# Keys of layers 2 and 3 stored with 32 rows per head and loaded in one piece per four heads; one batch's expert rows placed behind the other batch's norm

## The chip, the cores and the metric

One core of one Trainium2 chip runs the whole program. The metric is the device time in microseconds (us) of one execution; the time of a kernel is the median of three runs. Engines: PE (TensorE, matrix products), DVE (VectorE), ACT (ScalarE), POOL (GpSimd), SP (SyncE, which issues most DMA transfers). Each engine works through its own queue in order. 16 DMA engines move data between DRAM and the on-chip memory SBUF.

## The reference, cut to what matters

The network has four layers. Each adds a cross attention to a context of 2 x 1024 rows and then a feed-forward part to the residual rows `x` (2 batches of 512 rows of 256). The places of this change are layer 1's experts, layer 2's attention and layer 3's attention:

```python
x = x + tanh(g_xattn[1]) * L1_xattn(layernorm(x), ctx, ctx, ...)   # "attention 1": 16 heads of 8
x = x + tanh(g_ffn[1])   * L1_ffn(layernorm(x), Wg, bg, W1, W2)    # 8 experts, each row to one
x = x + tanh(g_xattn[2]) * L2_xattn(layernorm(x), ctx, ctx, ...)   # "attention 2": 16 heads of 16
x = x + tanh(g_ffn[2])   * L2_ffn(layernorm(x), ...)               # ternary weights
x = x + tanh(g_xattn[3]) * L3_xattn(layernorm(x), ctx, ctx, ...)   # "attention 3": 8 heads of 4
x = x + tanh(g_ffn[3])   * L3_ffn(layernorm(x), ...)
# an attention: softmax(q k^T * scale) v Wo, with q from layernorm(x) and k, v from ctx
```

## The kernel before, in words

The kernel is written in a tile framework. The program is traced as Python runs; a planner then puts the instructions of each engine in order, by what it reckons to be ready and by program order, gives buffers out and adds the semaphores. `keep_in_program_order` pins one instruction behind the one traced before it on the same engine; without it the planner may move it.

**Keys.** All keys are computed from the context ahead of their layer (`keys`, line 923) and written to DRAM tensors `K_l1`, `K_l2`, `K_l3` of shape [heads, head size + 1, 2048] (`prepare_context`, line 910). The extra row holds ones: the maximum of a score row is subtracted by way of it. An attention reads four heads at a time as a tile `KT` of 128 partitions x 2048 (`loaded_keys`, line 1013): head h of the four sits on partitions 32 h to 32 h + head size, and the rest must be zero. So `KT` is set to zero on POOL (line 1019), and four loads on SP (line 1021) bring the heads: 9 rows of 8 KB each for layer 1, 17 for layer 2, 5 for layer 3. There are 4, 4 and 2 such tiles.

`KT` lives in the buffers with the tag `wide`, of which there are four. The experts' weights `w1e` and `w2e` (1 MB each, lines 1306 and 1308) use the same four buffers, and the ternary part keeps half of its lowest split part and `w3` in them. A `KT` of layer 2 is therefore free to be filled only when the last experts have used their weights: the first when expert 6 is done with its first weight, the last at the end of the experts' last product.

**Experts.** `moe_ffn` (line 1300) sends each row to a place in DRAM by expert (`xg`, an indirect DMA from POOL), runs the experts one after another (`arrive`, `hidden`, `leave`; the output rows `ye` go from ACT's queue to `yg` in DRAM, line 1408), and asks for `KT` of layer 2 after the last. The rows come back in `rest` (line 1424), which attention 2 calls for each batch: four gathers from `yg` on POOL (line 1427), then four updates of `x` on DVE (line 1434).

**The start of an attention** (`attention`, line 1038). Batch 0's `rest` runs first. Then `queries(0)` and batch 1's `rest` are interleaved, one step of each in turn: `queries` begins with the row statistics (lines 156 to 168: statistics and aggregate per block on DVE, variance plus epsilon, square root on ACT, reciprocal and `nb` on DVE); the normalised rows `h` (line 184, ACT) are transposed on PE (line 1070), copied, and multiplied by the query weights (line 1076). Scores (line 1143), their maxima (DVE, lines 1150 and 1152), exponentials (1174, 1179) and values (1186) follow, group by group of four heads. `queries(1)` runs between the first scores.

**Attention 1's aside.** `prepare_routing` (line 1516) is called inside attention 1 after its first scores. It sets a tile `zero` (128 x 256) and stores it from SP over parts of `xg` and `yg` (2.5 MB, line 1524).

**The ternary part** (`ternary_ffn`, line 1582) calls `loads()` near its end: `KT` and values `V` of layer 3 (two loads of 1 MB, line 1032). Then comes a branch (line 1689) past a path in full precision that is not taken with these weights; every engine goes through it. Two more such branches are at lines 254 and 1364.

The interleaving that matters for the order of the updates:

```python
for _ in before(range(BPB), bank):
    pass
first, second = queries(0), before(range(BPB, NB), bank)
for _ in first:
    next(second, None)
for _ in second:
    pass
```

Of the kernel before, what the change touches and what calls it, by code (L numbers as in the profile page):

```python
# [20 lines left out]
F32 = mybir.dt.float32  # L21
# [4 lines left out]
ALU = mybir.AluOpType  # L26
# [3 lines left out]
B, S, D = 2, 512, 256  # L30
M = 1024
# [43 lines left out]
def _bc(ap, shape):  # L75

    return ap.broadcast_to(shape)


class _Net:  # L80
# [829 lines left out]
    def prepare_context(self):  # L910
        nc = self.nc
        self.kd, self.vd = {}, {}
        for name, H, HD in (("l1", 16, 8), ("l2", 16, 16), ("l3", 8, 4)):
            k = self.dram.tile([H, HD + 1, B * M], F32, name=f"K_{name}")
            self.kd[name] = k
            nc.sync.dma_start(
                k[:, HD, :].rearrange("h (c m) -> h c m", m=P),
                _bc(self.ones[:H].unsqueeze(1), [H, B * M // P, P]),
            )
        for name, H in (("l1", 16), ("l3", 8)):  # L920
            self.vd[name] = self.dram.tile([B * M, H * 32], F32, name=f"V_{name}")
# [88 lines left out]

        return V, self.by_key(wv, D, to), keys()

    def loaded_keys(self, name, H, HD):

        nc = self.nc
        KT = []
        for g in range(H // 4):
            k = self.wide("KT")([P, B, M])
            nc.gpsimd.memset(k, 0.0)  # L1019
            for h in range(4):  # L1020
                nc.sync.dma_start(
                    k[32 * h : 32 * h + HD + 1].rearrange("r b m -> r (b m)"),
                    self.kd[name][4 * g + h],
                )
            KT.append(k)
        return KT

# [10 lines left out]
    def attention(  # L1038
        self, name, KT, V, H, HD, scale, gate, before, bq=None, bv=None, bo=None, aside=None
    ):  # L1040
# [88 lines left out]
        def largest(u, ring=False):  # L1129
# [11 lines left out]
            for i in range(2):  # L1141
                r = 32 * (2 * pair + i)
                nc.tensor.matmul(  # L1143
                    sc[i], lhsT=QT[r : r + 32, g, (b * BPB + k) * P : (b * BPB + k + 1) * P],
                    rhs=KT[g][r : r + 32, b, ts(half, 512)], start=True, stop=True,
                )
# [153 lines left out]
    def moe_ffn(self, gate):  # L1300
        nc, d = self.nc, self.d
# [14 lines left out]
        rows = self.big.tile([P, NB, D], F32, tag="q", name="rows_h")  # L1316
        hT = self.hp.tile([P, DC, T], F32, tag="hT", name="hT")
        for n2 in range(NB // 2):
            tp = self.ps1.tile([P, DC, 2, P], F32, tag="one", name="tp")
            for k in range(2):  # L1320
                n = 2 * n2 + k
# [7 lines left out]
        p, dest, some, many = self.gates(gate, hT, wg, values)  # L1329
# [68 lines left out]
        def leave(e, h1, w2):  # L1398
            for t in range(2):
                ps = self.ps1.tile([HCAP, D], F32, tag="one", name="py")  # L1400
                for fc in range(HC):
                    nc.tensor.matmul(  # L1402
                        ps, lhsT=h1[:, fc, ts(t, HCAP)], rhs=w2[:, fc, :],
                        start=(fc == 0), stop=(fc == HC - 1),
                    )
                y = self.big.tile([HCAP, D], F32, tag="avj", name="ye", bufs=2)
                self.copy(y, ps)
                nc.scalar.dma_start(self.yg[e * CAP + t * HCAP : e * CAP + (t + 1) * HCAP], y)
# [10 lines left out]
            if e + 1 < NE and e + 1 not in ws:  # L1419
                ws[e + 1] = load(e + 1)  # L1420
        leave(*before)
        KT = self.loaded_keys("l2", 16, 16)

        def rest(blocks, bank):
            y = self.big.tile([P, BPB, D], F32, tag="e", name="yn", bufs=4)
            for k, n in enumerate(blocks):
                nc.gpsimd.indirect_dma_start(
                    out=y[:, k, :],
                    out_offset=None,
                    in_=self.yg[:, :],  # L1430
                    in_offset=bass.IndirectOffsetOnAxis(ap=dest[:, n : n + 1], axis=0),
                )
            for k, n in enumerate(blocks):
                nc.vector.scalar_tensor_tensor(
                    self.x[:, n, :], y[:, k, :], some[:, n : n + 1], self.x[:, n, :],
                    ALU.mult, ALU.add,
                )
                yield

# [76 lines left out]
    def prepare_routing(self):  # L1516

        nc = self.nc
        self.xg = self.dram.tile([NE * CAP + T, D], F32, name="xg")
        self.yg = self.dram.tile([NE * CAP + T, D], F32, name="yg")  # L1520
        zero = self.wk.tile([P, D], F32, tag="h", name="zero", bufs=2)
        nc.gpsimd.memset(zero, 0.0)
        for to, k in ((self.xg[: NE * CAP], NE * CAP // P), (self.yg[NE * CAP :], T // P)):
            nc.sync.dma_start(
                to.rearrange("(k p) f -> p k f", p=P), _bc(zero.unsqueeze(1), [P, k, D])
            )
        self.rank, self.first, self.behind = (
            self.const.tile([P, n], F32, name=name)
            for n, name in ((NE, "rank"), (NE, "first"), (NB, "behind"))
        )  # L1530
        for to, n, step, base, by in (
            (self.rank, NE, -1, NE, 0), (self.first, NE, CAP, 0, 0), (self.behind, NB, P, NE * CAP, 1)
        ):
            i = self.sm.tile([P, 8], I32, tag="ri", name="ri", bufs=1)
            nc.gpsimd.iota(i, pattern=[[step, n]], base=base, channel_multiplier=by)
            nc.vector.tensor_copy(to, i)

        self.upper = self.const.tile([P, P], F32, name="upper")
        nc.gpsimd.memset(self.upper, 1.0)
        nc.gpsimd.affine_select(  # L1540
            out=self.upper, in_=self.upper, pattern=[[1, P]], compare_op=ALU.is_gt, fill=0.0,
            base=0, channel_multiplier=-1,
        )
# [260 lines left out]
    def run(self):  # L1804
        ov = self.out.rearrange("(n p) f -> p n f", p=P)
        self.setup()
        self.sampled_attention()
        self.after_layer_0()
        kv = self.loaded_keys("l1", 16, 8), self.loaded_values("l1", 16)
        self.attention(  # L1810
            "l1", *kv, 16, 8, D**-0.5, 1, lambda blocks, bank: self.int8_ffn(4, blocks),
            aside=self.prepare_routing,
        )
        *kv, rest = self.moe_ffn(5)
        self.attention("l2", *kv, 16, 16, 0.25, 2, rest, "bq2", "bv2", "bo2")
        kv, rest = self.ternary_ffn(
            6, lambda: (self.loaded_keys("l3", 8, 4), self.loaded_values("l3", 8))
        )
        scale = float(np.float32(1.0) / np.sqrt(np.float32(32.0)))
        self.attention("l3", *kv, 8, 4, scale, 3, rest, "bq3", "bv3", "bo3")  # L1820
        self.channel_mix_ffn(
            7, lambda n: self.nc.sync.dma_start(ov[:, n, :], self.x[:, n, :])
        )
# [105 lines left out]
```

## Time and profile before

| | us |
|---|---|
| median of 3 runs (lowest, highest) | 1298.85 (1297.12, 1301.19) |
| the profiled execution | 1298.23 |
| its span | 1296.5 |
| PE busy in the span | 1156.7 (89%) |
| DVE, ACT, POOL busy | 720.3, 607.5, 228.3 |
| mean granted PE clock | 0.933 |
| `KT` memsets on POOL | 10 of 1.8 each |

The profile is of one execution: a span, the busy time of each engine, and groups of instructions by line with their mean duration and the idle time before them, with what ended it. A timeline lists instructions with start, duration, engine, line and tiles, and in brackets the idle time of the engine just before with its releaser. "out<-in" names tiles. A letter q behind an engine (SPq, PEq) is that engine's sequencer. In the tables by stretches of time each engine has its busy time in us and, in brackets, the instructions; then come the granted PE clock (1.00 is full), the busy share of the 16 DMA engines and GB/s.

### The profile page before, as it was taken

How to read it: one execution, taken by the hardware profiler on the slowest of the kernel's cores; microseconds unless marked ns; L12 is line 12 of the kernel's file. 1: busy time of each engine (PE TensorE's matmuls, PEld its weight loads, DVE VectorE, ACT ScalarE, POOL GpSimd, SP SyncE). 2: the span in 40 equal slices, each digit the busy share in tenths (PEclk: the TensorE clock that was granted, in tenths of full speed). 3: DMA queues.
4: the chain of work that ended last, by engine and by line, in shares of the span. 5: the costliest groups of instructions: out<-in, count | busy, mean ns of one | idle time of the engine just before them, and what ended most of it. 6: DMA issues, size and time to landing. Idle time of an engine off the chain costs nothing. (4 is left out here: it accounts for less than half of the span.)

```text
span 1296.5 us, 16857 instructions
## 1 busy us (share of the span) xinstructions
PE 1156.7 (89%) x6576; PEld 540.6 (42%) x6596; DVE 720.3 (56%) x1106; ACT 607.5 (47%) x1166; POOL 228.3 (18%) x204
## 2 busy tenths in 40 slices
PE   6987499999998989937999899969999997999977
PEld 3334333333334578823333233334444445543324
DVE  5794678787764111114788778448333111588635
ACT  2422236888874311103488678646333110258761
POOL 1043201334320200131033233000000000113200
PEclk9978698999999989977899999979999998989988
DMA  6033530000211345420000100000122112000000
GB/s 220 1 118 111 116 137 5 1 1 1 66 34 41 111 155 190 156 68 27 16 2 1 66 1 2 17 18 1 34 84 58 58 33 80 9 1 1 10 0 33
DMA packets 56837, 67.49 MB, mean 52 GB/s; under 512 B 4064, under 2 KB 45568, under 8 KB 56288
## 3 DMA queue, kind: packets, MB, share of 16 engines
q1 hardware_dynamic: 52856, 61.07, 15.0%
q0 software_dynamic: 896, 2.49, 0.7%
q10 hardware_dynamic: 2992, 2.70, 0.6%
q8 instruction: 57, 0.93, 0.3%
q14 instruction: 36, 0.29, 0.1%
HBM read 49.93 MB, written 16.32 MB: 51 GB/s over the span
## 5 line engine op out<-in xcount | busy, mean ns | idle before, releaser
L1152 DVE TENSOR_REDUCE part<-scores 128x2 f32<-128x1024 f32 x290 | 341.8, 1219 | 92.5 <-PE bank L1174 77.1
L1179 ACT ACTIVATE e<-bank 128x512 f32<-128x512 f32 x580 | 302.2, 601 | 121.1 <-PE bank L1174 89.4
L1174 PE MATMUL bank<-qa,KT 32*128 32x512 f32 x1160 | 306.1, 634 | 0.6 <-DVE o L1213 0.6
L1143 PE MATMUL scores<-KT,QT 32*128 32x512 f32 x1160 | 293.9, 641 | 4.2 <-DVE part L1152 4.2
L1198 POOL TENSOR_TENSOR avT<-avT,avj 128x512 f32<-128x512 f32 x113 | 143.2, 1268 | 345.9 <-ACT avj L1197 345.9
L1186 PE MATMUL bank<-e,V 128*32 128x512 f32 x1280 | 182.8, 607 | 2.5 <-ACT e L1179 2.5
L1143 PEld LDWEIGHTS scores<-KT,QT 32*128 32x128 f32 x1160 | 100.6, 190 | 157.3 <-DVE part L1152 115.3
L1634 PE MATMUL pg<-hid,wg_h 128*128 128x512 bf16 x752 | 165.1, 379 | 0.8
L1174 PEld LDWEIGHTS bank<-qa,KT 32*128 32x128 f32 x1160 | 117.2, 188 | 36.0 <-issue 18.2
L1634 PEld LDWEIGHTS <-wg_h 128*128 128x128 bf16 x768 | 75.1, 98 | 90.6
L1019 POOL MEMSET KT<- 128x2048 f32 x10 | 18.0, 1821 | 375.9 <-PE pg L1634 157.3
L1186 PEld LDWEIGHTS bank<-e,V 128*32 128x32 f32 x1280 | 28.3, 108 | 106.2 <-ACT e L1179 94.9
L1197 ACT COPY avj<-bank 128x512 f32<-128x512 f32 x113 | 69.2, 612 | 6.7 <-PE bank L1186 6.7
L1402 PE MATMUL py<-w2e,h 128*96 128x256 f32 x256 | 57.4, 379 | 0.0
L1596 DVE TENSOR_REDUCE low<-wg_h 128x1 f32<-128x1024 uint16 x16 | 19.5, 1217 | 57.1 <-DMA wg_h<-in_h2T 54.4
L1606 DVE TENSOR_TENSOR rest<-g,hid 128x512 f32<-128x512 f32 x32 | 21.2, 690 | 51.5 <-ACT hid L1605 51.3
L1070 PE MATMUL bank<-ident,h 128*128 128x128 f32 x48 | 11.7, 369 | 39.0 <-ACT h L184 32.2
L1402 PEld LDWEIGHTS py<-w2e,h 128*96 128x96 f32 x256 | 41.2, 163 | 12.2
L1386 PE MATMUL ph<-xeT,w1e 128*128 128x192 f32 x256 | 45.1, 337 | 0.0
L1386 PEld LDWEIGHTS ph<-xeT,w1e 128*128 128x128 f32 x256 | 43.6, 198 | 1.3 <-DVE xeT L109 0.6
L1076 PE MATMUL bank<-hT,w_l_wq 128*128 128x512 f32 x80 | 41.4, 644 | 2.1 <-DVE part L1150 1.4
L1667 ACT ACTIVATE hid<-pg,cols 128x512 f32<-128x512 f32 x16 | 10.1, 683 | 70.2 <-PE pg L1634 70.2
(303 smaller groups left out, 1325.2 us busy)
## 6 DMA issues: line engine op xcount, KB each, us to landing
w1e<-in_W SPq DMA_DIRECT2D x8, 1024.0 KB
w2e<-in_W SPq DMA_DIRECT2D x8, 1024.0 KB
V_l<-v1st SPq DMA_DIRECT2D x16, 256.0 KB
V<-V_l SPq DMA_DIRECT2D x2, 2048.0 KB
wg_h<-in_h1T SPq DMA_DIRECT2D x8, 512.0 KB
wg_h<-in_h2T SPq DMA_DIRECT2D x8, 512.0 KB
K_l<-kst SPq DMA_DIRECT2D x12, 256.0 KB
KT<-K_l SPq DMA_DIRECT2D x16, 136.0 KB
```

Of the source, the lines that this page charges most:

```text
L1076: nc.tensor.matmul(ps, lhsT=wq[:, dc, ts(c, P)], rhs=hT[:, dc, ts(b, S)], start=(dc == 0), stop=(dc == DC - 1),)
L1143: nc.tensor.matmul(sc[i], lhsT=QT[r : r + 32, g, (b * BPB + k) * P : (b * BPB + k + 1) * P], rhs=KT[g][r : r + 32, b, ts(half, 512)], star ...
L1152: nc.vector.tensor_reduce(to, both, AX.X, ALU.max, negate=True)
L1174: nc.tensor.matmul(t, lhsT=KT[g][r : r + 32, b, ts(j, P)], rhs=augmented[n][r : r + 32, :], start=True, stop=True,)
L1179: nc.scalar.activation(e[:, h, :], t, AF.Exp, scale=scale)
L1186: nc.tensor.matmul(po[32 * h : 32 * h + 32, :], lhsT=V[b][:, j, ts(4 * g + h, 32)], rhs=e[:, h, :], start=True, stop=True,)
L1197: nc.scalar.copy(t, po)
L1198: nc.gpsimd.tensor_tensor(part["oT"], part["oT"], t, ALU.add)
L1386: nc.tensor.matmul(ps[:, k // 2, k % 2, :CAP], lhsT=w1[:, dc, ts(4 * fp + k, P)], rhs=xeT[:, dc, :], start=(dc == 0), stop=(dc == DC - 1),)
L1402: nc.tensor.matmul(ps, lhsT=h1[:, fc, ts(t, HCAP)], rhs=w2[:, fc, :], start=(fc == 0), stop=(fc == HC - 1),)
L1606: nc.vector.tensor_tensor(r, g, hi, ALU.subtract)
L1634: nc.tensor.matmul(ps[:, ts(t, 512)], lhsT=w[:, c, ts(oc, P)], rhs=src(i, c, ts_(t, 512)), start=(c == 0 and i == 0), stop=(c == chunks - ...
```

## The change

Layers 2 and 3 get 32 rows per head in DRAM, so that four heads are 128 rows that lie one behind another: one load of 1 MB fills a whole `KT`, and the memset goes. The rows that were zeroed in SBUF before are now stored as zeros in DRAM, once, by three stores in `prepare_routing`, inside attention 1. Layer 1 stays as it was. Besides, the updates of batch 1 in the experts' `rest` are pinned in program order, which puts the first of them behind the last DVE instruction of batch 0's statistics (`nb`, line 168) and each other one behind the one before.

```diff
@@ prepare_context
-            k = self.dram.tile([H, HD + 1, B * M], F32, name=f"K_{name}")
+            rows = HD + 1 if name == "l1" else 32
+            k = self.dram.tile([H, rows, B * M], F32, name=f"K_{name}")
@@ loaded_keys
-    def loaded_keys(self, name, H, HD):
+    def loaded_keys(self, name, H):
...
             k = self.wide("KT")([P, B, M])
-            nc.gpsimd.memset(k, 0.0)
-            for h in range(4):
-                nc.sync.dma_start(
-                    k[32 * h : 32 * h + HD + 1].rearrange("r b m -> r (b m)"),
-                    self.kd[name][4 * g + h],
-                )
+            kd = self.kd[name][4 * g : 4 * g + 4]
+            flat = k.rearrange("p b m -> p (b m)")
+            if kd.shape[1] == 32:
+                nc.sync.dma_start(flat, kd.rearrange("h r m -> (h r) m"))
+            else:
+                nc.gpsimd.memset(k, 0.0)
+                for h in range(4):
+                    nc.sync.dma_start(flat[32 * h : 32 * h + kd.shape[1]], kd[h])
             KT.append(k)
@@ moe_ffn, rest
+            stay = self.tc.keep_in_program_order if blocks.start else lambda i: i
             for k, n in enumerate(blocks):
-                nc.vector.scalar_tensor_tensor(
-                    self.x[:, n, :], y[:, k, :], some[:, n : n + 1], self.x[:, n, :],
-                    ALU.mult, ALU.add,
+                stay(
+                    nc.vector.scalar_tensor_tensor(
+                        self.x[:, n, :], y[:, k, :], some[:, n : n + 1], self.x[:, n, :],
+                        ALU.mult, ALU.add,
+                    )
                 )
                 yield
@@ prepare_routing
+        for name, HD in (("l2", 16), ("l3", 4)):
+
+            for h in range(0, self.kd[name].shape[0], 8):
+                to = self.kd[name][h : h + 8, HD + 1 :, :]
+                nc.sync.dma_start(
+                    to.rearrange("h r m -> h (r m)").rearrange("h (c m) -> h c m", m=D),
+                    _bc(zero[:8].unsqueeze(1), [8, (31 - HD) * B * M // D, D]),
+                )
```

More of the change, by code (lines that the diff above doesn't have):

```diff
@@ L1421, in moe_ffn @@
         leave(*before)
-        KT = self.loaded_keys("l2", 16, 16)
+        KT = self.loaded_keys("l2", 16)
         def rest(blocks, bank):
@@ L1808, in run @@
         self.after_layer_0()
-        kv = self.loaded_keys("l1", 16, 8), self.loaded_values("l1", 16)
+        kv = self.loaded_keys("l1", 16), self.loaded_values("l1", 16)
         self.attention(
@@ L1816, in run @@
         kv, rest = self.ternary_ffn(
-            6, lambda: (self.loaded_keys("l3", 8, 4), self.loaded_values("l3", 8))
+            6, lambda: (self.loaded_keys("l3", 8), self.loaded_values("l3", 8))
         )
```

## The prediction

> **What bounds the kernel now.** I read the page first. TensorE (PE) is busy for 89% of a span of 1296.5 us; the program is a chain of stages on one core, and PE is the engine that ends most of them. So a change that touches no matmul can pay only where PE stands still. The slices show one such place outside the start: around 565 to 585 us, between the experts and attention 2. I took the timelines of each engine there, then the stretches of 1 us.
>
> PE's timeline: after the experts' last product (562.0) PE starts again with the transposes of attention 2's normalised rows.
>
> ```profile
> 587.31 1.18 PE L1070 MATMUL bank<-ident,h 128*128 128x128 f32 x4 [25.32 <-ACT h L184]
> ```
>
> 25.3 us are empty. What is in them, from the timelines of POOL, SP, DVE and ACT (start, duration, engine, line):
>
> ```profile
> 562.05 1.80 POOL L1019 MEMSET KT<- 128x2048 f32 x1 [5.10 <-PE py L1402]
> 569.92 1.05 POOL L1427 DMA_INDIRECT yn<-yg,gt  x1 [6.07 <-DMA KT<-K_l]
> ```
> ```profile
> 579.63 0.48 DVE L1434 SCALAR_TENSOR_TENSOR x<-yn,gt,x 128x256 f32<-128x256 f32 x1 [0.82 <-DMA yn<-yg,gt]
> ...
> 581.23 0.45 DVE L1434 SCALAR_TENSOR_TENSOR x<-yn,gt,x 128x256 f32<-128x256 f32 x1
> 581.60 0.17 DVE L157 BATCH_NORM_AGGREGATE mv<-st 128x2 f32<-128x6 f32 x1
> 581.92 0.48 DVE L1434 SCALAR_TENSOR_TENSOR x<-yn,gt,x 128x256 f32<-128x256 f32 x1
> 582.32 0.16 DVE L160 TENSOR_SCALAR rs<-mv 128x4 f32<-128x4 f32 x1
> 583.53 0.48 DVE L1434 SCALAR_TENSOR_TENSOR x<-yn,gt,x 128x256 f32<-128x256 f32 x1 [1.05 <-DMA yn<-yg,gt]
> 584.81 0.48 DVE L1434 SCALAR_TENSOR_TENSOR x<-yn,gt,x 128x256 f32<-128x256 f32 x1 [0.79 <-DMA yn<-yg,gt]
> ...
> 586.26 0.16 DVE L162 RECIPROCAL rs<-rs 128x4 f32<-128x4 f32 x1
> ...
> 586.48 0.14 DVE L168 SCALAR_TENSOR_TENSOR nb<-mv,rs 128x4 f32<-128x4 f32 x1
> ```
> ```profile
> 582.52 0.20 ACT L161 ACTIVATE rs<-rs 128x4 f32<-128x4 f32 x1 [18.42 <-DVE rs L160]
> 586.65 1.09 ACT L184 ACTIVATE h<-x,nb,rs 128x256 f32<-128x256 f32 x2 [3.93 <-DVE nb L168]
> ```
>
> Two holes are to be seen. POOL stands for 6.07 us before the first gather of expert rows, on a load of keys that the gather does not read. And ACT has the root of batch 0's variance at 582.72, but its reciprocal runs at 586.26: in front of it on DVE stand four updates of batch 1's rows (581.23 to 585.29), the last two waiting for gathers.
>
> Why the keys are slow, from the stretches of 1 us (after the engines: PE clock, DMA share, GB/s): the first is all keys, the second a weight load of 1 MB.
>
> ```profile
> 566.00:567.00 1.00, 0.00 (x0) 0.00 (x0) 0.00 (x0) 0.00 (x0) 0.00 (x0) 1.00 0.06 27
> ...
> 540.00:541.00 1.00, 1.00 (x6) 0.74 (x5) 0.00 (x0) 0.00 (x0) 0.00 (x0) 1.00 1.08 384
> ```
>
> A load of 17 rows (136 KB) fills 0.06 of the DMA engines, one of 16, at 25 to 27 GB/s: 5.3 us each, one after another. SP's issues agree (568.79, then 574.07). The 1 MB load was issued at 536.57 and its traffic is over at 542.0: 5.4 us.
>
> **The change, part by part.**
>
> *Zeros in attention 1.* Three more stores on SP behind those issued at 178.6 and 179.0: 16 heads x 15 rows x 8 KB + 8 x 27 x 8 KB = 3.7 MB, in pieces of 1 KB, out of 8 partitions. The existing zeros (2.5 MB, same pieces, 128 partitions) took 9 us, at 386 GB/s at best. Bounds: 14 us at that rate, 150 us if they went through one engine like the 17-row loads; so over by 195 to 330. Behind them on SP are a value weight (192.57; needed near 400) and expert weights (326). The moved transfers otherwise stay, and attention 1's DMA is idle (0 to 2 GB/s from 200 to 300). Cost: 0, cover over 70 us.
>
> *Keys of layer 2.* Gone: 4 memsets of 1.80 us on POOL and 16 loads of 136 KB; new: 4 loads of 1 MB straight behind the release of their buffers (542.4, 549.0, 555.1, 562.0). The first three land inside the experts' 12.5 us rhythm (two 1 MB weights each did so without delay for PE); the bytes double to 4 MB, and the scores that want the first group start only at 600.73. The fourth is issued at about 562.1 and lands at 562.1 + 5.4 = 567.5.
> The gather then waits for the last expert rows alone. Their store is issued at 562.5; its traffic shows at 563 to 564 (0.38 of the engines, 112 GB/s), and POOL's first semaphore wait ends at 564.7. Behind the event that ends POOL's hole (568.9) the gather started 1.0 us later, so without rivals in the queue it would start at 565.7. But the fourth key load now shares all 16 engines with that store. Bounds: 565.7 (no loss) and 568.5 (the store ends with the key load); taken 566.5, nearer to the first, since 96 KB in 1 us alone stretch to about 2 us at half the rate. Gain 569.9 - 566.5 = 3.4 us (1.4 to 4.2).
> The gathers take 5.8 us each from issue to landing, beside the keys on one engine; the scatter of the same rows took 3.6. I keep 5.8; the end of the key queue could give 2.2 more.
>
> [...]
>
> *Batch 1's rows behind batch 0's norm.* The pinned updates now stand on DVE behind line 168's `nb`. From the last update of batch 0 (579.63) the order left is: aggregate, statistics x2, aggregate, statistics, two aggregates (to 581.47 by their rows, the two updates at 581.23 and 581.92 taken out), `rs` 0.16, root on ACT 0.20, reciprocal 0.18, `nb` 0.14, with 0.05 to 0.1 between engines: `nb` ends at about 582.2 and ACT's `h` starts at 582.3, not 586.65: gain 4.3 us. Queued behind the waiting updates are batch 1's statistics (finished at 588.2 before, wanted by transposes at 604.9): about 1.5 us later against `h`, with 10 us to spare, unless ACT's queue puts their root early (below).
>
> *Keys of layer 3.* Gone 2 memsets and 8 loads of 40 KB; 2 loads of 1 MB instead. The first goes at 962.4 between 1 MB of w3 and a weight issued at 971.7: room for 2 x 5.4 us; cost 0. The second starts at 1070.2, when its buffer is free (the memset held it until 1072.0), and is over by 1075.6; the two value loads go out at 1074.5 and fill the engines to 1083. That matters: PE's branch past the skipped full-precision path took 7.7 us (1076.1 to 1083.8), while the branch at line 254, with quiet DMA, took 3.6. I read it as code fetched beside those loads. The key load's tail pushes them by 0 to 0.7 MB, at 350 GB/s 0 to 2.0 us; taken 0.4 loss.
>
> *Sum.* -3.4 - 4.3 + 0.4 = -7.3 us, all of it in PE's hole, which shrinks from 25.3 to about 17.6 us, less the 0.4 at layer 3. What is late next is the gather itself (issue of four, 5.0 us, and 5.8 to land). The clock does not add to it: it fell to 0.5 at 567.6, 5.6 us into the hole, and was full 7.3 us after PE's restart; a hole of 17.6 us falls and recovers alike. The profiled run took 1298.23 (span 1296.5), the median is 1298.85; I set the sum against the median, 0.6 above its own run: 1291.5.
>
> **Rivals.**
> [...]
> 2. *ACT's queue gives the second gain back.* Today batch 1's root (587.65) stands between the second and third `h`. If it stays there it now waits for batch 1's last update (5.2 us behind batch 0's last) plus statistics, about 3.8 us behind `nb`, where the third `h` started 1.6 behind it: 2.4 us lost, sum -4.9: 1294. If the planner also leaves statistics of batch 0 late, little of the second part is left: 1296. Against: the planner orders by readiness, and the pin makes that root late.
> 3. *The change doesn't reach the path:* the gather still waits for a key load because its wait counts transfers that share a counter. [...]
> 4. *Slower: the zeros starve code loading in attention 1.* The page's row of 57 instruction loads, 0.93 MB, makes 16 KB each; 16857 instructions in 1.22 MB make about 226 in each, and PE issues 332 in 20 us there, so one load per 14 us. If each were as late as at the branch (7.7 instead of 3.6, uncovered 4.1 us), zeros that run 14 us cost 4 us, and those that run the bound of 150 us cost 11 x 4.1 = 45. It decides from 62 us on (18 us lost against 7.3 won: 1309.5). Against: from 180 to 185 the engines were at 1.09 of their share and PE was busy 4.63 of 5.00; beside the expert weights 10.0 of 10.0.
>
> **Chances.** Forecast (-6 to -10 us) 0.60; more, by faster gathers, 0.08 (1287.5); rivals 1 and 3 0.13; rival 2 0.13; rival 4 0.06. What a measurement can tell from no change is 0.3%, 3.9 us: below 1294.95 is faster. Forecast, the more, rivals 1 and 3 mostly, and a third of rival 2 lie there: 0.81; within 0.13, slower 0.06. The range takes in the faster gathers (-3.4 - 2.2 - 4.3 - 0.8 for the best start, -10.7 or 1288, a little below for the clock) and rival 2's worse end: 1287 to 1297.
>
> **What would show it.** First gather at 566 to 567, with no key load named before it; `nb` within 3 us of batch 0's last update, batch 1's updates behind it; PE's hole 16 to 19 us; the key loads as four issues of 1024 KB with a share near 1.0; PE's branch at line 1689's place 7.5 to 9.5 us; attention 1 from 200 to 400 unchanged. I am wrong if the hole shrinks as said but attention 1 or the branch grew, or if the gather waits on the fourth key load beyond 568.5.

## The result, and the profile after

| | before | after |
|---|---|---|
| median of 6 runs, us (lowest, highest) | 1300.02 (1297.12, 1301.56) | 1289.57 (1285.61, 1292.14) |
| ratio, 95% interval | | 0.9925 (0.9900 to 0.9951) |
| profiled execution, us | 1298.23 | 1286.37 |
| its span | 1296.5 | 1284.6 |
| PE empty between experts and attention 2 | 25.3 | 16.3 |

Faster by 0.75%, with the whole interval below 1; inside the range, and 1.9 us under the forecast of 1291.5. Measured once more (below) the change stood at 0.9956 (0.9932 to 0.9980), so its size is 0.4 to 0.75%, not better known than that. Ratios here and below compare a kernel with the kernel before of the same round of measurement; the ratio isn't that of the medians, so the two can differ by 0.15%.

PE's timeline after: the restart behind the experts, to be held against the line of before with 25.32 in brackets. (Line numbers have moved by three to fifteen.)

```profile
576.39 1.18 PE L1073 MATMUL bank<-ident,h 128*128 128x128 f32 x4 [16.26 <-ACT h L184]
```

POOL's timeline, the first gather: it now names the store of the last expert rows, and stands at 566.40; the experts' product ended at 560.13 in this execution (561.99 before), so it is 6.3 us behind it, 7.9 before.

```profile
566.40 1.04 POOL L1430 DMA_INDIRECT yn<-yg,gt  x1 [118.88 <-DMA yg<-ye]
```

DVE's timeline, in the order that the pin gives: batch 0's last update, its statistics without a hole, `nb` (line 168), and only then batch 1's updates.

```profile
573.04 0.48 DVE L1440 SCALAR_TENSOR_TENSOR x<-yn,gt,x 128x256 f32<-128x256 f32 x1 [0.74 <-DMA yn<-yg,gt]
...
575.55 0.16 DVE L168 SCALAR_TENSOR_TENSOR nb<-mv,rs 128x4 f32<-128x4 f32 x1
575.63 0.87 DVE L1440 SCALAR_TENSOR_TENSOR x<-yn,gt,x 128x256 f32<-128x256 f32 x2
```

From 573.04 to `nb` are 2.5 us; before, from 579.63 to 586.48, 6.9. The first update ran at 569.20, 2.8 us behind its gather's start; before 5.75.

ACT's timeline shows what came in place of it: batch 1's root (580.44) waits 1.69 us for batch 1's variance, and batch 0's second copy `hT` stands behind it.

```profile
580.44 0.20 ACT L161 ACTIVATE rs<-rs 128x4 f32<-128x4 f32 x1 [1.69 <-DVE rs L160]
580.55 0.57 ACT L1074 COPY hT<-bank 128x512 f32<-128x512 f32 x1
```

Where the time went, by stages, from the starts of the same lines in both executions (us; the last column is from the first value load of layer 1 to the last output store):

```
                 first V load | to experts' end | to attention 2's bias product | to ternary products | to w3 products | to channel mix | whole
before                  138.9 |           422.7 |                          38.2 |               262.8 |          221.5 |          186.4 | 1154.5
after                   137.3 |           422.5 |                          30.9 |               261.3 |          222.8 |          184.0 | 1144.3
```

The rest of the whole, 22.9 and 22.8, is the channel mix itself. 7.3 us come from the stage that the change aims at; 2.7 from the three stages behind it, where only layer 3's keys are loaded in another way; and 1.6 from the opening, whose code is the same.

### The profile page after: what moved, and what is told of

The parts are those of the page before. It is cut to its first block, busy times and chain, and to the rows that moved or that the text cites. A ratio compares the mean times of both kernels' runs of the same rounds, so it can differ in the third digit from the quotient of the medians.

```text
span 1284.6 us, 16809 instructions
## 1 busy us (share of the span) xinstructions
PE 1152.8 (90%) x6576; PEld 538.0 (42%) x6596; DVE 720.9 (56%) x1106; ACT 607.7 (47%) x1166; POOL 217.4 (17%) x198
## 5 line engine op out<-in xcount | busy, mean ns | idle before, releaser
L1146 PE MATMUL scores<-KT,QT 32*128 32x512 f32 x1160 | 290.1, 632 | 4.4 <-DVE part L1155 4.4
L1201 POOL TENSOR_TENSOR avT<-avT,avj 128x512 f32<-128x512 f32 x113 | 143.3, 1268 | 343.4 <-ACT avj L1200 343.4
L1153 DVE TENSOR_REDUCE part<-bank 128x1 f32<-128x512 f32 x60 | 37.4, 682 | 3.8 <-PE bank L1146 3.4
```

What stands on the lines that cost most here:

```text
L1146: nc.tensor.matmul(sc[i], lhsT=QT[r : r + 32, g, (b * BPB + k) * P : (b * BPB + k + 1) * P], rhs=KT[g][r : r + 32, b, ts(half, 512)], star ...
L1153: nc.vector.tensor_reduce(to[:, i : i + 1], sc[i], AX.X, ALU.max, negate=True)
L1201: nc.gpsimd.tensor_tensor(part["oT"], part["oT"], t, ALU.add)
```

## The experiments

Theory: two gains that add, both in PE's hole. The keys on all DMA engines let the gathers start and land earlier; the pin takes batch 1's updates out of batch 0's norm. Rivals: the pin does all, the keys do all, the zeros cost something elsewhere. In the table below "hole" is PE's idle time behind the experts, "gather" the first gather's start behind the experts' end, "landing" from there to the first update, "scores" the first scores behind the experts' end, "stage" the time from the experts' end to attention 2's bias product; these five are of one profiled execution each. "Median" is the median less that of the kernel before of the same round.

```
                    gather  landing  hole  scores  stage   median   ratio to before (95%)
before                7.9     5.8    25.3   38.8    38.2
after                 6.3     2.8    16.3   31.5    30.9    -10.5    0.9925 (0.9900-0.9951)
keys only             6.1     2.9    20.3   34.5    33.9     -4.1    0.9973 (0.9947-0.9998)
pin only              7.9     5.8    21.0   35.6    35.0     -3.4    0.9967 (0.9948-0.9985)
zeros only            7.8     6.0    25.1   38.6    38.1     +2.6    1.0034 (1.0010-1.0058)
split rows, pin       3.2     6.1    18.8   32.1    31.5     -6.3    0.9952 (0.9930-0.9974)
last load late        3.2     2.8    13.2   28.0    27.4     -9.6    0.9931 (0.9904-0.9958)
root pinned           6.2     2.9    16.3   30.3    29.7     -4.8    0.9955 (0.9933-0.9977)
both of these         3.2     2.9    13.1   27.3    26.7    -12.9    0.9896 (0.9865-0.9927)
zeros thrice          6.2     2.8    16.2   31.1    30.6     +5.0    1.0026 (1.0005-1.0047)
no zeros              3.2     4.9    15.9   30.5    29.9     -8.0    0.9932 (0.9911-0.9954)
change again          6.1     2.9    16.2   31.4    30.8     -4.5    0.9956 (0.9932-0.9980)
both again            3.2     2.8    13.2   27.8    27.2     -6.3    0.9943 (0.9919-0.9966)
```

**Keys only.**

```diff
-            stay = self.tc.keep_in_program_order if blocks.start else lambda i: i
+            stay = lambda i: i
```

> The whole change without the pin: 32 rows per head, zeros in attention 1, one load per four heads. Theory (two additive gains in PE's hole between experts and attention 2: the gather starts 1.7 us earlier against the experts' last product and lands in 2.8 instead of 5.8 us, 4.7 together, and the pin gives 4.3 more, of which ACT's queue returns about 1): the gathers land in 2.8 us, batch 0's nb again stands behind batch 1's updates, PE's hole is 20.5 us (25.3 before, 16.3 with all of it), the time 4 to 6 us under the kernel before. Rival A (the pin does all): hole 24 to 25, time as before. Rival B (the keys do all and the pin nothing): hole 16 to 17, time 8 to 11 us under before.

PE's timeline of that kernel:

```profile
581.51 1.18 PE L1073 MATMUL bank<-ident,h 128*128 128x128 f32 x4 [20.28 <-ACT h L184]
```

Hole 20.28 us, gathers landing in 2.9, `nb` again behind batch 1's updates; ratio 0.9973. As the theory had it.

**Pin only**, on the kernel before:

```diff
+            stay = self.tc.keep_in_program_order if blocks.start else lambda i: i
             for k, n in enumerate(blocks):
-                nc.vector.scalar_tensor_tensor(
+                stay(nc.vector.scalar_tensor_tensor(
...
```

> The kernel before with the pin alone. Theory: gathers start 7.9 us behind the experts' last product and land in 5.8 us as before; nb follows batch 0's last update by 2.5 us instead of 6.9; hole 21 us; time 3 to 4.5 us under the kernel before. Rival A: 8 to 11 us under. Rival B: as before.

PE's timeline of that kernel:

```profile
589.67 1.18 PE L1070 MATMUL bank<-ident,h 128*128 128x128 f32 x4 [21.02 <-ACT h L184]
```

25.3 to 21.0, gathers as before: 4.3 us. The keys alone gave 5.0 us; together 9.1 of 9.3. The two add (in the stage 3.1 and 4.3, together 7.3), and both rivals that give all to one of them fall.

**Zeros only**: DRAM with 32 rows and the zeros, but the old loads and memsets, no pin.

```diff
...
-                nc.sync.dma_start(flat, kd.rearrange("h r m -> (h r) m"))
...
+            rows = {"l1": 9, "l2": 17, "l3": 5}[name]
+            nc.gpsimd.memset(k, 0.0)
+            for h in range(4):
+                nc.sync.dma_start(flat[32 * h : 32 * h + rows], kd[h, :rows])
```

> The kernel before with 32 rows per head in DRAM and the zeros stored in attention 1, but with the old memsets and the old loads of 9, 17 and 5 rows, and no pin: what the zeros cost alone. Theory: nothing, within 2 us of the kernel before; PE's hole 25 us; the value weight behind the zeros on SP goes out at about 240 instead of 193. Rival (the zeros slow code loading or attention 1): 2 to 6 us over before, and attention 1 between 180 and 400 longer by as much.

The time came out at 1.0034, some 4 us over by the ratio and 2.6 by the median, where the rival had it; the profile did not. A stretch of 20 us in attention 1, of this kernel:

```profile
220.00:240.00 20.00, 19.71 (x168) 6.97 (x160) 16.10 (x17) 16.41 (x33) 7.04 (x6) 1.00 0.42 52
```

and of the kernel before:

```profile
220.00:240.00 20.00, 19.71 (x164) 7.35 (x168) 15.79 (x17) 16.12 (x32) 6.44 (x6) 1.00 0.01 2
```

PE is as busy with the zeros going (0.42 of the engines, 52 GB/s) as without. From the first value load to the experts' end the kernel took 423.0 us, before 422.7; in all from there 1154.7 against 1154.5. But the profiled execution (1296.79 us) was the third fastest of twelve, whose median is 1299.63; what the slower ones lost, and where, no trace shows. So the zeros were enlarged later.

**Split rows**: the kernel before with the pin, its 17-row loads cut in two.

```diff
-                nc.sync.dma_start(k[32 * h : 32 * h + HD + 1]..., self.kd[name][4 * g + h])
+                cuts = (0, 16, 17) if HD == 16 else (0, HD + 1)
+                for a, z in zip(cuts, cuts[1:]):
+                    nc.sync.dma_start(k[32 * h + a : 32 * h + z]..., self.kd[name][4 * g + h, a:z])
```

> The kernel before with the pin, the old memsets and the old DRAM layout, but each 17-row load cut into one of 16 rows and one of the single row of ones: no zeros in DRAM, no load of 1 MB. Theory (the old loads were slow only because 17 rows go to one DMA engine, and that engine is what delayed the gathers): the 16-row loads use all engines, the gathers land in about 3 us, hole 16 to 18 us, time as with the whole change, 8 to 11 us under before. Rival (the memsets or the number of loads are what cost, or the bytes per load): hole 20 to 22, time like the pin alone, 3 to 5 us under before.

Half of the theory came out. The first gather started 3.2 us behind the product, earlier than with the change and as early as without memsets (last load late, below), so the memsets are no cost there. But the gathers were slow and uneven; DVE's timeline of this kernel:

```profile
575.28 0.48 DVE L1438 SCALAR_TENSOR_TENSOR x<-yn,gt,x 128x256 f32<-128x256 f32 x1 [8.85 <-DMA yn<-yg,gt]
...
577.53 0.48 DVE L1438 SCALAR_TENSOR_TENSOR x<-yn,gt,x 128x256 f32<-128x256 f32 x1 [1.30 <-DMA yn<-yg,gt]
579.91 0.49 DVE L1438 SCALAR_TENSOR_TENSOR x<-yn,gt,x 128x256 f32<-128x256 f32 x1 [1.90 <-DMA yn<-yg,gt]
```

Updates 2.3 us apart, where they were 1.3 apart before: the small key loads run beside the gathers (DMA share 0.7 to 1.2 from 570 to 582 in this kernel). Even so the stage took 31.5 us, 0.7 more than with the change, and the time (0.9952) is that of the change measured again: most of the gain needs neither 32 rows in DRAM nor zeros. The run also said that the change's own gather, at 6.3, was held by something that split loads do not do. That led to the next one.

**Last load late**: the whole change, with the fourth load of layer 2's keys issued behind the gathers and dependent on batch 1's last one (`last`).

```diff
+            if name == "l2" and g == 3:
+                self.held = flat, kd.rearrange("h r m -> (h r) m")
...
+            if blocks.start:
+                load = nc.sync.dma_start(*self.held)
+                self.tc.add_manual_dep(load.ins, last.ins.name, ...)
```

> The whole change, with the fourth key load of layer 2 sent only when batch 1's last gather has landed. Theory (the 1 MB load that is issued as the experts' last product ends shares the DMA engines with the last expert rows' store, and delays its landing by some 3 us: the first gather stood at 6.3 us behind the product, where the split loads had it at 3.2): the first gather starts 3.2 to 4 us behind the product, lands in 2.8 to 3.5, PE's hole falls from 16.3 to 13 to 14 us; the time is 2 to 3 us under the whole change, 10 to 13 under the kernel before. Rival (what holds the gather is the store's own latency or the gather's start on POOL): first gather still at 6 us, hole 16, time as the whole change.

The timelines of POOL and PE:

```profile
563.90 1.04 POOL L1432 DMA_INDIRECT yn<-yg,gt  x1 [115.64 <-DMA yg<-ye]
```
```profile
573.88 1.18 PE L1075 MATMUL bank<-ident,h 128*128 128x128 f32 x4 [13.15 <-ACT h L184]
```

The gather at 3.2 us, the hole at 13.2: the fourth load had cost 3.1 us. Of the gain in the stage (3.4 us to the bias product) the whole program shows nothing in this execution: 1144.2 from the first value load, 1144.3 after the change. Attention 2 took 263.7 us instead of 261.3.

**Root pinned**: the whole change, batch 1's root in attention 2 pinned on ACT.

```diff
+        root = nc.scalar.activation(r, r, AF.Sqrt)
+        if in_order or pin_root:
+            self.tc.keep_in_program_order(root)
...
+            stats = self.statistics(range(...), pin_root=name == "l2" and b == 1)
```

> The whole change, with batch 1's square root in attention 2 pinned behind batch 0's copies and query copies on ACT. Theory (after the change ACT waits 1.7 us for batch 1's variance between batch 0's third normalised row block and its second copy, and PE waits as long for that copy): the second copy comes 1.0 to 1.2 us earlier against PE's restart, the first scores at 30.3 us behind the experts' last product instead of 31.5; time about 1 us under the whole change, less than the measurement tells. Rival (PE's clock, at half speed there, sets the time to the first scores): scores at 31.5 as before.

The second copy came 1.0 us earlier and the first scores at 30.3 instead of 31.5 behind the product, with the same hole of 16.3: what the prediction's second rival named is real, at 1.2 us, not its 2.4. The time (0.9955) tells nothing of so little.

**Both**, and **both again** beside the change.

> The last key load late and the root pinned, together. Theory: the two gains add, first scores 27 to 28 us behind the experts' last product (31.5 in the whole change, 38.8 before), time 11 to 14 us under the kernel before. Rival (the earlier restart is taken back by the half clock, whose stretches come in steps of 3.4 us): scores at 28 to 30, time no better than the whole change.

> The last load late and the root pinned, once more beside the change. Theory: 3 to 5 us under the change, 11 to 15 under the kernel before. Rival (the gain over the change is scatter): within 2 us of the change.

> The change itself once more, on the same chip as the two beside it. Theory: 8 to 11 us under the kernel before. Rival (the first measurement was lucky, the profile's hole is partly taken back): 4 to 7 under.

Scores at 27.3 and 27.8, as added up. In time 0.9896 at first and 0.9943 when run beside the change (0.9956): the version is below both kernels in every median, but by 1.8 us beside the change, with intervals that overlap. So that part of the theory's expectation (3 to 5 us) is not confirmed in time, only in the stage. The change itself, again, fell by 4.5 us, with the same hole (16.2) and the same stage (30.8 us): there the rival's figure came out.

**Zeros thrice.**

```diff
-        for name, HD in (("l2", 16), ("l3", 4)):
+        for name, HD in 3 * (("l2", 16), ("l3", 4)):
```

> The whole change with every zero stored three times, 11.2 MB instead of 3.7: what the zeros cost, enlarged. Theory (nothing: the zeros lie in attention 1, where nobody needs the DMA; the 0.3% by which the zeros alone stood above the kernel before is scatter of the runs' first 140 us): SP is busy with them until about 365 us, the first expert weight goes out that late and is still in time; attention 1 from 180 to 410 as long as before, time as the whole change within 2 us. Rival (62 us of zeros cost 4 us): 8 to 10 us over the whole change, and attention 1 longer by that.

The theory was wrong by its numbers: 1.0026 to before, 5 us over it in the median, where the change was 10.5 and 4.5 us under it. SP's timeline shows one way:

```profile
180.24 175.48 SPq L1538 DMA_DIRECT2D K_l<-zero  x9
355.77 34.30 SPq L1309 DMA_DIRECT2D w1e<-in_W  x1
...
405.33 3.56 SPq L120 DMA_DIRECT2D w_wv<-in_wv  x1
```

The zeros ran to about 390, the queue behind them was late, and the value weight left at 405 instead of 193 (208 with the change), when its products were due. PE's timeline:

```profile
417.46 2.90 PE L954 MATMUL pv<-w_wv,ctxT 128*128 128x256 f32 x6 [5.96 <-DMA w_wv<-in_wv]
```

There is a second way, inside attention 1. A stretch of 20 us, first of this kernel and then of the kernel after the change, and PE's timeline of this kernel in it:

```profile
300.00:320.00 20.00, 17.67 (x137) 5.65 (x132) 14.36 (x14) 14.84 (x29) 7.66 (x7) 1.00 0.42 52
...
300.00:320.00 20.00, 18.86 (x160) 6.63 (x156) 15.05 (x16) 15.78 (x31) 8.34 (x8) 1.00 0.00 1
```
```profile
319.69 1.06 PE L1189 MATMUL bank<-e,V 128*32 128x512 f32 x6 [0.76 <-issue]
```

PE stops here, and for 0.45 us at 300.9, without waiting for anything that the profile shows ("issue"). Counted from the first value load and held against the change instruction by instruction, this execution is even to 0.1 us up to 300, 1.1 late at 304 and 2.9 late at 322. The trace has loads of instructions (the DMA queue q8 of the profile) at 298.6, 317.3 and 320.8, right beside the two stops. That makes code loading among the zeros the likely cause; it is not shown.

So of the 7.5 us that were lost by the experts' end (430.0 against 422.5), 2.9 arose in attention 1 and 4.6 where the value weight was missing: the queue behind the zeros on SP is the larger part, due only when they outlast the slack. With the zeros stored once no such delay is in the profiles: before, after and zeros only stay within 0.2 us of one another from the first value load to 430.

**No zeros**: the kernel before with split rows, the pin, the last tile's loads late and the root pinned.

> The kernel before (memsets, old DRAM layout, no zeros stored) with the pin, the 17-row loads cut into 16 rows and 1, the last tile's loads sent behind batch 1's gathers, and batch 1's root pinned on ACT. Theory (rows per load and the moment of the last load are all that counts; 32 rows in DRAM, the zeros and the missing memsets are not needed): first gather at 3.2 us behind the experts' last product, landing in 2.8 to 3, PE's hole 13.2, first scores at 27.3 as with both edits on the whole change; time 11 to 14 us under the kernel before. Rival (many small loads on SP are still going when the gathers run): gathers land in 5 to 8 us as with the split loads, hole 16 to 19.

The rival came out. The gather started at 3.2, but landing took 4.9 and more, and the hole was 15.9. What SP waited for in these 50 us, from its waits (total, number, longest):

```profile
SPq L1033 <- DMA yg<-ye: 12.9, 4, 4.3
```

Key loads waited four times for stores of expert rows that they have nothing to do with, so 11 of the 24 loads went out only from 566.0 on, amid the gathers. The trace has both under the same semaphores: eight counters of landing (100 and 102 to 108 in the trace of before) go round among the transfers of SP and ACT, and a load waits until the one before it on its counter has landed (before, a load on counter 107 goes out at 563.05, and the landing on it stands at 563.03). With one load for four heads these loads (line 1023 after the change) wait for PE and once for ACT, and for no transfer. So in the stage the 32 rows earn 2.7 us by the count of loads (27.2 against 29.9), not by the memset. In time that does not show: on the same chip no zeros gained 8.0 us in the median (0.9932), both again 6.3 (0.9943) and the change 4.5 (0.9956), with intervals that overlap.

## Why the prediction was right

**The sum.** -7.3 was forecast, -7.7 of it in the stage behind the experts and +0.4 at layer 3. The stage went from 38.2 to 30.9, -7.3, and to 30.8 when repeated; layer 3 gave +0.1. That this agrees to 0.1 us is in part luck: inside the stage the gather's start gave 1.7 less than forecast, its landing 2.9 more, and ACT's queue and PE's half clock took back 1.0 and 0.8. The medians fell by 10.5 and by 4.5 us; between them lies scatter, most of which the change does not make (below).

**The gather's start** was mis-sized: 3.4 us forecast, with 566.5, that is 4.5 behind the product; measured 6.3, a gain of 1.7. That the gather stood at 566.40, where the signs wanted it, is no proof: this execution was 1.9 us early at the experts' end. The later of the prediction's two bounds, 568.5 (the store ends with the key load; its chances count this as rivals 1 and 3), is 6.5 behind the product, and was right about the gather. Stretches of 1 us after the change:

```profile
561.00:562.00 1.00, 0.00 (x0) 0.00 (x0) 0.00 (x0) 1.00 (x1) 0.00 (x0) 1.00 1.04 147
...
564.00:565.00 1.00, 0.00 (x0) 0.00 (x0) 0.00 (x0) 0.00 (x0) 0.00 (x0) 0.50 0.80 312
565.00:566.00 1.00, 0.00 (x0) 0.00 (x0) 0.00 (x0) 0.00 (x0) 0.00 (x0) 0.50 0.02 7
```

Key load and store are issued 0.5 us apart (560.17 and 560.63); POOL's semaphore events stand at 565.5, when the key load is over, though 90 of the store's 96 pieces of 1 KB moved between 563.29 and 563.82 before. The trace's list of DMA pieces has no piece of the store ahead of 564.35, and the last of the key load ends at 564.88. With that load away the gather starts at 3.2. Why no piece of the store moves earlier beside the 1 MB load, while in the kernel before single pieces of store and keys take turns on one engine (next paragraph), is not shown.

**What the gather waited for before** the prediction read wrongly: it was not a key load, but the store of the last expert rows itself. In these traces the semaphore of such a store is raised sixteen times, once for each sixteenth of it. Before, fifteen raises came by 2.2 us behind the product (564.15) and the sixteenth at 6.9 (568.92), 1.0 us ahead of the gather; its last six pieces of 1 KB moved between 566.46 and 568.20, each between two 8 KB pieces of keys. Pin only and zeros only show the same (6.9 and 7.0). After the change all sixteen come between 4.8 and 5.4 us; with split rows or the last load late, all by 2.2. So one DMA engine busy with 17-row loads held a sixteenth of the store to 6.9 us, and the 1 MB load held all of it for a shorter time, to 4.8 to 5.4. The name of a key load in the profile is inferred from a semaphore that serves both.

**The landing** was mis-sized the other way: 5.8 us kept, 2.8 measured, 2.9 gained; the text had offered 2.2 as a bonus. Pin only (5.8, old keys) against keys only (2.9) puts it on the key queue, and the semaphores say how: before, fifteen raises of each of batch 0's gathers come within 2.9 us of its start and the sixteenth at 5.7 to 5.8; after, all sixteen within 2.8. That batch 0's updates came evenly before, 1.3 us apart (575.67, 576.99, 578.32, 579.63), does not speak against a held transfer: each gather was held in one sixteenth. The misses of start and landing cancel to 1.2 us.

**The pin**: 4.3 forecast, 4.3 measured alone (25.3 to 21.0). **ACT's queue**: 0 forecast, 1.2 measured by pinning the root; rival 2's mechanism at half its price (the wait in front of the first query product grew from 0.68 to 1.68). The rest of the difference between hole (-9.1) and stage (-7.3) stands in the query products at the half clock: 9.63 us for the 16 after, 8.86 before. The claim that the clock "falls and recovers alike" was too smooth: it fell to 0.5 5.3 us into the hole before (not 5.6) and 2.2 after, and was full again 7.3 us behind the restart before, 9.8 after. So a hole that is 9.1 us shorter made the stretch at half clock only 3.4 shorter (27.3 and 23.9). In the clock records of these two executions every stretch at 0.50 except the last is 3.41 us long or a multiple of that (3.41 to 27.31).

**Layer 3's keys**: 0.4 forecast. PE's branch took 7.8 us instead of 7.7, and its wait 8.8 instead of 8.7: 0.1.

**The zeros**: cost 0 was forecast. The profiles agree at this size, the time leaves it open (zeros only, 1.0010 to 1.0058). The three kernels without zeros (pin only, split rows, no zeros) gained in the median what their stage gained, to 0.4 us; of the eight with the zeros stored once, six fell short of it by 0.2 to 4.7 and two gained 1.4 and 3.2 more. That would fit a cost of the zeros in some executions, and does not show it. Their run was bounded by 14 and 150 us; the engines were at 0.42 until 255 and at rest from 260, and the last piece ended at 257.8, so it took some 79 us from the first issue, the value weight behind them taken in. They moved at 52 GB/s, 0.42 of the engines, against 386 for the existing zeros, which come out of 128 partitions. That the number of partitions makes this difference is not shown: no run varied it alone. Rival 4 (code loading) would by its own price (4.1 us per 14) have cost 23 us with a run of 79; at this size the profiles show none of it. With three times the zeros 2.9 us in attention 1 may be its work, so it is not excluded, only far smaller than its price.

**Behind the stage** nothing was forecast and 2.7 us appeared, 1.5 of it in attention 2 and 1.2 in the ternary stage and attention 3 together. Attention 2 took 260.4 to 265.0 us over the 13 profiles; with the very same code there it took 261.3, 261.4 and 264.5 (after, change again, zeros thrice), so the 1.5 can't be told from scatter. The 1.2 comes back: 408.0 and 407.8 before and with zeros only, 406.8, 406.7 and 406.7 in those three. It isn't layer 3's loads: last load late and both, where they are the same as in the change, took 407.3 to 407.8. Granted clock changes there between 0.50 and 1.00; that the place of its steps makes these differences is likely and not shown.

**What stays open.** The opening: the first value load of layer 1 stood between 137.3 and 143.3 us in the 13 profiles, with the same code ahead of it. From there to the experts' end, zeros thrice aside, the profiles took either 422.5 to 423.3 or 425.2 to 426.1 us, with zeros and without, and in the upper group the difference is there within 70 us of the value load; the change had 422.5 at first and 425.2 again. Such scatter is the size of the change, which is why stages tell here what medians cannot. And whether the zeros cost time in the executions that were not profiled.

## What to carry to other kernels

Look at what is in the DMA queues at the moment when the last product of a stage ends: here a load of 1 MB that this product releases was over (564.88) before the 96 KB store that the next stage waits for had landed (565.5), and holding it back by a dependence was worth 3.1 us of the hole (the time did not show it clearly). When an engine seems to wait for a transfer that its instruction does not read, look at when each share of the transfer that it does read has landed, and count the transfers in flight and their rows, since here both loads on one DMA engine (gathers landed in 5.8 us) and a swarm of small ones (6.1 with split rows) delayed their neighbours (2.8 after the change). And judge edits of less than 1% by the stage they touch, from a fixed line to a fixed line, beside the medians.

## What the runs showed of the hardware that was not expected

Loads of 17 rows of 8 KB ran at 25 to 27 GB/s on one engine. Beside them the last of sixteen shares of a 96 KB store landed 4.8 us behind the other fifteen, and that of a gather some 2.9 us, so gathers took 5.8 us instead of 2.8. A store of 96 KB that shares its start with a 1 MB load landed when the load was over, 3.2 us later than without it. Stores out of 8 partitions moved 52 GB/s. SP blocked on issuing the next transfer for 34 us while zeros stood ahead of it (34 us at 52 GB/s are 1.8 MB). SP's timeline of the kernel after the change, with the start of the issue and how long it took:

```profile
178.45 29.38 SPq L1538 DMA_DIRECT2D K_l<-zero  x3
207.93 34.05 SPq L120 DMA_DIRECT2D w_wv<-in_wv  x1
```
